# Attention and ternary feed-forward in one kernel: how h2's Strassen factors are made, when factors are fetched, and 96 bytes of padding

## The chip, the cores and the metric

The kernel runs on one core of a Trainium2 chip. A core has five engines that run their own instruction streams: TensorE (PE; its weight loads are shown as PEld), VectorE (DVE), ScalarE (ACT), GpSimd (POOL) and SyncE (SP, which here only issues DMAs). The metric is the device time of one execution in microseconds. Three runs of the kernel before gave 877.13, 877.68 and 878.19 us.

## The reference

The input x has 2 sequences of 2048 tokens with 256 features, all in fp32. The output is a residual sum of a causal attention and a feed-forward network, both on the normalised x:

```python
xn = layernorm(x)
q, k, v = xn @ Wq, xn @ Wk, xn @ Wv
attn = softmax(where(causal, q @ k.T, -max) * 256**-0.5) @ v @ Wo
h = silu((xn @ w1.T) * w1_s) * ((xn @ w2.T) * w2_s)      # 256 -> 1024
h = gelu((h @ h1.T) * h1_s)                              # 1024 -> 1024
h = gelu((h @ h2.T) * h2_s)                              # 1024 -> 1024
out = x + attn + (h @ w3.T) * w3_s                       # 1024 -> 256
```

The weights w1, w2, h1, h2 and w3 hold only -1, 0 and 1 in this input; their scales w1_s and so on are real numbers, one for each output feature.

## The kernel before, in words

**Blocks and passes.** The 4096 tokens are 8 blocks of 512. Attention comes first (to about 280 us). For each block it leaves two things in DRAM: xT_d, the normalised block with features on the partitions, split into a high and a low part so that two fp32r matmuls together are exact enough; and r_d, the attention's result. While it runs, it also looks through the feed-forward weights to see that they are ternary. If they are, ffn_ternary runs (L697), otherwise a general version (ffn) that the change leaves alone.

ffn_ternary goes over the blocks in pairs: four passes of an even block n and an odd block n + 1. The tile xh0 holds the even block's xn, xh1 (in the profile xh1t) the odd one's. xh0 is in the pool const, which is laid out first and stays for the whole kernel; xh1 is in a pool that is laid out after const, once attention's pools are gone, and so are the other tiles of ffn_ternary.

**One pass.** `first` (L728) computes the 1024 hidden features of both blocks as four quarters B11, B12, B22, B21: the first figure of the name picks the half of the features and the second the token block, so B11 and B21 use xh0, B12 and B22 use xh1. Each quarter has 4 tiles of 128 features by 512 tokens. For each tile PE makes two products of 4 matmuls (L741) in two PSUM banks, ACT applies silu (L746), DVE multiplies (L747), and what a later product needs is split into high and low parts by ACT (L724) and DVE (L725). The differences that Strassen's scheme (in Winograd's form) needs are made in t1 (L762, DVE), b22 (L767 on GpSimd, L768 on DVE) and later at L826 (GpSimd).

`square` (L773) then does a 1024 x 1024 layer with seven half-sized products instead of eight. The list STEPS (L39) gives for each of the seven the left factor, made of the weights, and the right one, made of the activations. The left factors of a layer lie in a DRAM tile, factors["h1"] and factors["h2"], as seven parts of 1 MB: part 0 is A11, parts 1 to 4 are the sums S1, S2, S4, S3, parts 5 and 6 are A12 and A22. A product fetches its factor into a tile w of a pool with three buffers (L781, L782) and runs 32 matmuls (L789). After h1 and h2 comes the last layer for both blocks (ps_y, L897), with the residual: rt (from r_d) and xt (from x) are loaded at L884 and L886 and added by GpSimd at L887.

**Making the factors of h2.** h1's factors are made during attention; of h2's weights, only the check of their values is done there. The parts of h2 are made in pass 1 by make_h2 (L852), once for each of 4 row groups c: two loads of 512 KB into the two staging tiles stgt (L856), four adds by GpSimd (L150) into a tile sums that has one buffer, and store_factors (L152): one store of the four sums (1 MB, L153) and three stores of 256 KB from the staging tiles (L154, L156) for the parts 0, 5 and 6, which are plain quarters of h2. load_w3 (L862) loads and rounds w3 in two halves. The list `later` holds these six steps in order; one is taken after B11, after B12, and after products 0, 2, 4 and 5 of the first layer (L756, L794).

**What sets the order.** The program is written in the order described, but a planner puts each engine's instructions into an order of its own: it estimates durations and gives an engine the earliest one in program order that it takes to be ready. Instructions that depend on nothing can so come far ahead of their place: rt and xt of pass 1 are issued at 287 us, though they belong at its end. On the chip each engine then works its own stream strictly in that order. All DMAs of ffn_ternary are issued by SP and so go into one queue.

## Time and profile before

| | |
|---|---|
| median of three runs | 877.68 us |
| the profiled execution | 877.43 us, its span 875.6 us |
| busy over the span | PE 854.3 us (98%), DVE 630.6 (72%), ACT 498.0 (57%), POOL 235.6 (27%) |
| feed-forward matmuls with xh / xh1t as moving operand (L741) | 256 each, 60.0 and 60.6 us busy |
| factor fetches (L782) | 56 of 1 MB, median 4.7 us from issue to landing |
| GpSimd's sums for h2 (L150) | 16, of 1.46 to 1.57 us on average |
| stores of h2's sums / of its quarters | 4 of 1 MB, median 8.0 us; 12 of 256 KB, median 5.9 us |

The profile is of one execution. Busy time of PE counts pipelined matmuls whose ends overlap, so that the pace of PE is read from the distance between starts, not from an instruction's duration. A timeline line gives start, duration of the group, engine, line, operation, output <- inputs, shapes and count; in square brackets how long the engine had sat idle before it and what is taken to have released it. Where that releaser had been done for long, the real one was something else, often a DMA.

### The profile page before, as it was taken

The numbers are of one execution on the slowest core, as the hardware profiler recorded it, in microseconds if no ns is written. First come the engines' busy times: TensorE is split into PE (matmuls) and PEld (weight loads), VectorE is DVE, ScalarE is ACT, GpSimd is POOL, SyncE is SP. The second block draws the span as 40 slices with busy tenths as digits, with TensorE's granted clock in tenths as the row PEclk, the third lists the DMA queues.
The fourth block names the chain that finished last, engine by engine and source line by source line (L and its number), as shares of the span: only waits on it lengthen the run. The fifth ranks groups of instructions, "written<-read, shape, count | busy, mean of one in ns | idle before, by whom it ended". The sixth has DMA issues, their size and how long they took to land.

```text
span 875.6 us, 12225 instructions
## 1 busy us (share of the span) xinstructions
PE 854.3 (98%) x4280; PEld 721.6 (82%) x4280; DVE 630.6 (72%) x1127; ACT 498.0 (57%) x881; POOL 235.6 (27%) x176
## 2 busy tenths in 40 slices
PE   8999999999998999999999999999999999999996
PEld 5888878988877877888988888888888898888886
DVE  5698689796873995985496596569468648848663
ACT  2546555754753664677266586536557635657670
POOL 4012533202121574440143050025024012502401
PEclk8999999999999999999999999999999999999998
DMA  8877599866892969744424444432434442144312
GB/s 305 326 229 242 168 321 293 302 236 200 238 325 91 365 239 378 258 147 145 139 90 146 147 144 145 156 125 99 144 144 145 147 142 97 49 144 145 144 49 77
DMA packets 63989, 162.51 MB, mean 186 GB/s; under 512 B 6704, under 2 KB 36528, under 8 KB 54704
## 3 DMA queue, kind: packets, MB, share of 16 engines
q1 hardware_dynamic: 58448, 145.92, 48.6%
q10 hardware_dynamic: 5472, 15.73, 5.6%
q8 instruction: 36, 0.59, 0.3%
q14 instruction: 33, 0.27, 0.1%
HBM read 117.06 MB, written 47.71 MB: 188 GB/s over the span
## 4 chain that ended last, share of the span: by engine, by line
PE 70%; DMA 13%; DVE 7%; issue 2%; ACT 2%; SPq 2%; POOL 2%; ACTq 0%; DVEq 0%; POOLq 0%
PE ps_h_X L789 26%; PE ps_w_B L741 13%; PE ps_h_Z L789 13%; PE ps_h_Y L789 7%; PE ps_y L897 6%; DMA e<-d 6%; DMA d<-b 4%; DMA stg<-in_ffn_h_w 2%; SPq L267 2%; DVE b L255 2%; PE pv L336 1%; PE po L443 1%; DVE stg L530 1%; POOL x L283 1%; DVE s L373 1%
## 5 line engine op out<-in xcount | busy, mean ns | idle before, releaser
L364 PE MATMUL pss<-k,q 128*128 128x512 f32 (+3 forms) x480 | 111.0, 369 | 3.1 <-DVE q L215 1.7
L364 PEld LDWEIGHTS pss<-k,q 128*128 128x128 f32 x480 | 81.8, 189 | 16.2 <-DVE q L215 2.1
L789 PE MATMUL ps_h_X<-h_h_T,w_h_S 128*128 128x512 f32 x384 | 89.0, 389 | 0.0
L789 PEld LDWEIGHTS ps_h_X<-h_h_T,w_h_S 128*128 128x128 f32 x384 | 72.1, 188 | 15.0
L443 PE MATMUL po<-v,pT 128*128 128x512 f32 x272 | 79.7, 405 | 3.0 <-ACT pT L423 1.9
L425 POOL TENSOR_TENSOR pT<-e,pT 128x512 fp32r<-128x512 f32 (+3 forms) x30 | 36.3, 1212 | 162.3 <-ACT pT L423 101.6
L887 POOL TENSOR_TENSOR rt<-rt,xt 128x1024 f32<-128x1024 f32 x8 | 19.7, 2458 | 216.5 <-DMA rt<-r_d 200.3
L810 ACT ACTIVATE k_h_u<-k_h_u,h_s_sb 128x512 f32<-128x512 f32 x64 | 46.1, 722 | 41.6 <-DVE k_h_u L809 41.4
L746 ACT ACTIVATE f_w_B<-ps_w_B,w_s_sb 128x512 f32<-128x512 f32 x64 | 42.8, 683 | 43.1 <-PE ps_w_B L741 43.1
L741 PE MATMUL ps_w_B<-xh,w_sb 128*128 128x512 f32 x256 | 60.0, 391 | 2.9 <-DVE f_w_B L747 1.6
L897 PEld LDWEIGHTS ps_y<-w_sbt,h_h_B 128*128 128x128 f32 x512 | 62.0, 192 | 0.3
L897 PE MATMUL ps_y<-w_sbt,h_h_B 128*128 128x256 f32 x512 | 62.1, 283 | 0.0
L423 ACT CAST pT<-e 128x512 fp32r<-128x512 f32 (+3 forms) x60 | 32.6, 573 | 49.6 <-DMA e<-d 38.3
L741 PE MATMUL ps_w_B<-xh1t,w_sb 128*128 128x512 f32 x256 | 60.6, 396 | 0.0
L789 PE MATMUL ps_h_Y<-h_h_B,w_h_A 128*128 128x512 f32 x256 | 59.3, 389 | 0.0
L789 PE MATMUL ps_h_X<-h_h_T,w_h_A 128*128 128x512 f32 x256 | 59.3, 389 | 0.0
L741 PEld LDWEIGHTS ps_w_B<-xh,w_sb 128*128 128x128 f32 x256 | 47.7, 188 | 13.4 <-DVE f_w_B L747 2.0
L443 PEld LDWEIGHTS po<-v,pT 128*128 128x128 f32 x272 | 49.0, 193 | 11.0 <-ACT pT L423 2.4
L741 PEld LDWEIGHTS ps_w_B<-xh1t,w_sb 128*128 128x128 f32 x256 | 48.1, 188 | 11.8
L789 PEld LDWEIGHTS ps_h_Y<-h_h_B,w_h_A 128*128 128x128 f32 x256 | 48.0, 188 | 10.0
L789 PEld LDWEIGHTS ps_h_X<-h_h_T,w_h_A 128*128 128x128 f32 x256 | 48.0, 188 | 10.0
L385 ACT ACTIVATE s<-s,low 128x1024 f32<-128x1024 f32 (+7 forms) x48 | 43.0, 898 | 21.3 <-DVE low L379 21.0
(139 smaller groups left out, 1845.3 us busy)
## 6 DMA issues: line engine op xcount, KB each, us to landing
w_h_S<-factors_h SPq DMA_DIRECT2D x32, 1024.0 KB, 4.7
w_h_A<-factors_h SPq DMA_DIRECT2D x24, 1024.0 KB, 4.7
d<-b SPq DMA_DIRECT2D x18, 512.0 KB, 4.3
e<-d SPq DMA_DIRECT2D x72, 128.0 KB, 4.1
xT_d<-k SPq DMA_DIRECT2D x8, 1024.0 KB, 8.7
stg<-in_ffn_h_w ACTq DMA_DIRECT2D x16, 512.0 KB, 6.5
x<-in_attn_x SPq DMA_DIRECT2D x16, 256.0 KB, 6.5
r_d<-r SPq DMA_DIRECT2D x8, 512.0 KB, 5.5
```

Source lines behind the costliest of these rows:

```text
L255: nc.vector.transpose(b.rearrange("p (g k q) -> p k g q", g=P // Q, q=Q), src.rearrange("p (k g q) -> p k g q", g=P // Q, q=Q),)
L364: nc.tensor.matmul(out=ps[:, :w], lhsT=qs[n][:, c, a, ts(t, P)], rhs=ks[m][:, c, b, :w], start=(k == 0), stop=(m < n and k == 3 * DC - 1),)
L385: marks["ACT"] = nc.scalar.activation(st["s"][:, at], st["s"][:, at], AF.Exp, bias=low, accum_out=st["sums"][:, u // UK : u // UK + 1],).ins
L423: nc.scalar.copy(hi, src)
L425: engine.tensor_tensor(lo, src, hi.bitcast(F32), ALU.subtract)
L443: nc.tensor.matmul(out=st["po"], lhsT=pT[:, 0, ts(j, P)], rhs=vs[m][:, j, :, :], start=(m == first and j == 0), stop=False,)
L741: nc.tensor.matmul(out=p, lhsT=w[:, c, ts(o, P)], rhs=xh[:, c, a, :], start=(c == 0 and a == 0), stop=(c == DC - 1 and a == 1),)
L746: nc.scalar.activation(f, p1, AF.Silu, scale=sc["w1"][:, o : o + 1])
L789: nc.tensor.matmul(out=out[o], lhsT=w[:, c, ts(o, P)], rhs=sets[right][c][:, a, :], start=(start and c == 0 and a == 0), stop=(c == HK - 1 ...
L810: nc.scalar.activation(C[k][o], r[o] if r else banks[o], AF.Gelu, scale=s[:, at : at + 1])
L887: nc.gpsimd.tensor_tensor(rest, rest, xt, ALU.add)
L897: nc.tensor.matmul(out=ys[t][:, :D], lhsT=h[c][:, a, ts(t, P)], rhs=w3_sb[:, c, :], start=(c == 0 and a == 0), stop=(c == HC - 1 and a == 1),)
```

## The change

Four things change, all but the first in ffn_ternary.

1. A tile of 24 floats per partition, named pad and used by nothing, is added at the end of const. Each tile laid out after const starts 96 bytes higher.
2. make_h2 stores the four sums only. The three plain quarters of h2 (parts 0, 5 and 6) are copied by copy_h2, one DMA of 1 MB each, from h2 in DRAM to factors["h2"] in DRAM, without a tile in between.
3. The steps sit at other places of pass 1, by name rather than in a list: make_h2(0) after B11, copy of part 0 after B12, make_h2(1) after B22, copy of part 5 after product 0 of h1, make_h2(2) after product 1, copy of part 6 after product 2, make_h2(3) after product 3, and the halves of w3 after products 5 and 6.
4. The factor tiles are fetched by fetch_factors, which keeps up to three of them asked for, across layers and passes. It is called once before pass 1, right after the load of xh1, and at the beginning of every product; a product takes the first of the list. In program order a fetch so stands two products ahead of its use. The pool still has three buffers.

```diff
     flag = const.tile([1, 1], I32, name="flag")
+    const.tile([P, 24], F32, name="pad")
...
-    def store_factors(f, c, sums, halves):
-        nc.sync.dma_start(out=f[:, 1:5, c, :], in_=sums)
-        nc.sync.dma_start(out=f[:, 0, c, :], in_=halves[0][:, :HB])
-        for i in range(2):
-            nc.sync.dma_start(out=f[:, 5 + i, c, :], in_=halves[1][:, ts(i, HB)])
...
-                if later and k in ("B11", "B12"):
-                    later.pop(0)()
+                beside(k)
...
-                left, right = STEPS[step]
-                w = wp.tile([P, HK, HB], F32R, tag="w", name=f"w_{name}_{left}")
-                nc.sync.dma_start(
-                    out=w.bitcast(F32).rearrange("p c o -> p (c o)"),
-                    in_=factors[layer][:, step].rearrange("p c o -> p (c o)"),
-                )
+                right = STEPS[step][1]
+                fetch_factors()
+                w = factor_tiles.pop(0)
...
-                if later and step in (0, 2, 4, 5):
-                    later.pop(0)()
+                if layer == "h1":
+                    beside(step)
...
-            store_factors(factors["h2"], c, sums, halves)
+            nc.sync.dma_start(out=factors["h2"][:, 1:5, c, :], in_=sums)
...
-        later = [lambda c=c: make_h2(c) for c in range(HK)]
+        def copy_h2(step):
+            k, o = {0: (0, 0), 5: (HK, 0), 6: (HK, HB)}[step]
+            nc.sync.dma_start(out=factors["h2"][:, step], in_=h2[:, ds(k, HK), ds(o, HB)])
+
+        later = {
+            "B11": lambda: make_h2(0), "B12": lambda: copy_h2(0), "B22": lambda: make_h2(1),
+            0: lambda: copy_h2(5), 1: lambda: make_h2(2), 2: lambda: copy_h2(6),
+            3: lambda: make_h2(3), 5: lambda: load_w3(0), 6: lambda: load_w3(SC // D),
+        }
+
+        def beside(at):
+            if at in later:
+                later.pop(at)()
+
+        factor_order = [
+            (layer, n, step) for n in range(0, N, 2) for layer in ("h1", "h2") for step in range(len(STEPS))
+        ]
+        factor_tiles = []
+
+        def fetch_factors():
+            while factor_order and len(factor_tiles) < 3:
+                layer, n, step = factor_order.pop(0)
+                w = wp.tile([P, HK, HB], F32R, tag="w", name=f"w_{layer}_{n}_{STEPS[step][0]}")
+                nc.sync.dma_start(
+                    out=w.bitcast(F32).rearrange("p c o -> p (c o)"),
+                    in_=factors[layer][:, step].rearrange("p c o -> p (c o)"),
+                )
+                factor_tiles.append(w)
+
         load_xh(1)
-        for c in range(0, HC, SC // D):
-            later.append(lambda c=c: load_w3(c))
+        fetch_factors()
```

More of the change, by code (lines that the diff above doesn't have):

```diff
@@ L865, in load_w3 @@
             rounded(w3_sb[:, c : c + SC // D, :].rearrange("p c d -> p (c d)"), t)
-        later = [lambda c=c: make_h2(c) for c in range(HK)]
+        def copy_h2(step):
[6 more added lines that the diff above has]
+        }
+        assert HK == 4 and HC == 2 * SC // D
+        def beside(at):
[14 more added lines that the diff above has]
+                factor_tiles.append(w)
         load_xh(1)
-        for c in range(0, HC, SC // D):
-            later.append(lambda c=c: load_w3(c))
+        fetch_factors()
         for n in range(0, N, 2):
```

## The prediction

> **What bounds the kernel now.** I read the page's header first, then the busy times by stage, then the chain that ended last, and then, where that chain leaves TensorE, the timelines of the engines concerned. The stages of the answer by windows are attention, the four passes of the feed-forward half (two token blocks each), and the tail; the columns are window, length, busy time and instruction count of PE, PEld, DVE, ACT, POOL, then clock, DMA share and GB/s.
>
> ```profile
> 0.00:279.70 279.70, 267.48 (x1464) 227.77 (x1465) 213.77 (x551) 151.40 (x297) 72.33 (x86) 0.98 0.78 251
> 279.70:429.00 149.30, 147.27 (x705) 123.55 (x706) 110.49 (x139) 87.56 (x147) 60.48 (x36) 1.00 0.68 247
> 429.00:575.50 146.50, 146.50 (x705) 123.49 (x705) 101.58 (x145) 86.72 (x146) 34.68 (x19) 1.00 0.39 137
> 868.50:875.60 7.10, 0.03 (x1) 0.00 (x0) 1.63 (x5) 0.00 (x0) 0.00 (x0) 0.68 0.24 81
> ```
>
> From 279.7 to 868.5 us TensorE sets the time: passes 2 to 4 have no idle PE at all and take 146.5 each. Pass 1 takes 149.3, of which PE is idle 2.03. So there are two things to win in this half: those 2 us, and the pace of single matmuls. The change touches neither attention's instructions nor the tail.
>
> The pace is read from the start times in PE's timeline of pass 2:
>
> ```profile
> 428.84 7.46 PE L741 MATMUL ps_w_B<-xh,w_sb 128*128 128x512 f32 x32
> 436.14 15.15 PE L741 MATMUL ps_w_B<-xh1t,w_sb 128*128 128x512 f32 x64
> 451.13 7.44 PE L741 MATMUL ps_w_B<-xh,w_sb 128*128 128x512 f32 x32
> 458.41 7.46 PE L789 MATMUL ps_h_X<-h_B,w_h_A 128*128 128x512 f32 x32
> 465.70 7.42 PE L789 MATMUL ps_h_Z<-h_T,w_h_S 128*128 128x512 f32 x32
> 472.96 1.30 PE L789 MATMUL ps_h_X<-h_T,w_h_S 128*128 128x512 f32 x5
> ```
>
> The same shape costs (472.96-465.70)/32 = 227 ns in the products, (436.14-428.84)/32 = 228 with the even block's xh as moving operand, but (451.13-436.14)/64 = 234 with the odd block's xh1t. Nothing waits there; the only difference is the tile.
>
> The two stalls of pass 1, from the timelines of PE, POOL, DVE and SP's queue:
>
> ```profile
> 310.19 1.21 PE L741 MATMUL ps_w_B<-xh,w_sb 128*128 128x512 f32 x4 [1.62 <-DVE f_w_B L747]
> ...
> 333.57 7.54 PE L789 MATMUL ps_h_Z<-h_B,w_h_S 128*128 128x512 f32 x32 [0.39 <-ACT h_h_T L724]
> ```
>
> ```profile
> 301.42 2.87 POOL L887 TENSOR_TENSOR rt<-rt,xt 128x1024 f32<-128x1024 f32 x1 [6.32 <-PE ps_w_B L741]
> 304.24 4.69 POOL L767 TENSOR_TENSOR f_w_B<-f_w_B,f_w_B 128x512 f32<-128x512 f32 x3
> ```
>
> ```profile
> 302.60 2.24 DVE L725 TENSOR_TENSOR h_B<-f_w_B,h_B 128x512 fp32r<-128x512 f32 x1
> 306.02 1.76 DVE L768 TENSOR_TENSOR f_w_B<-f_w_B,f_w_B 128x512 f32<-128x512 f32 x1 [1.19 <-POOL f_w_B L767]
> ```
>
> ```profile
> 323.99 0.37 SPq L153 DMA_DIRECT2D factors_h<-sums_h  x1
> 324.47 0.45 SPq L856 DMA_DIRECT2D stgt_h<-in_ffn_h_w  x1
> 325.00 0.98 SPq L782 DMA_DIRECT2D w_h_S<-factors_h  x1
> ```
>
> The first stall runs backwards so. PE lacks a PSUM bank until L747 has read it (309.40 to 310.14). That multiply stood behind L768, which waits for GpSimd's L767. L767 could have begun when f_w_B was there (302.69), but began at 304.24, because the residual add L887 was ahead of it on POOL. The add's wait is put down to PE, but its xt was issued at 287.48 and took 13.8 us to land, so 301.3: it was the DMA. The queue is full there (392 GB/s between 287 and 302, DMA share 1.00). The second stall is also a DMA: the step's matmul had its banks since 323.3, and ACT is a coincidence; its factor w (S4) was issued at 325.0 and took 8.4 us, so 333.4. The slot was free at 318.5, when product 0 ended; SP stood behind the store of h2's second sums, which waited for GpSimd until 323.99.
>
> **What the Trainium skill says.** "TensorE: Matmul & The Clock Gate", Step-by-step: PE has two independent SBUF read ports, and loading the next weights takes no bandwidth from the running matmul. The trace does not quite agree: 234 against 227 ns. The built addresses of the kernel before are the hint: w1_sb at byte 16512 and xh0 at 32896 are multiples of 64; xh1t at 50464 is 32 past one. In the products both operands are 32 past one, and they run at 227: slow is the mixed pair, not the odd address. "SBUF — State Buffer", SBUF: two separate sides: DVE and GpSimd share a port pair as an exclusive lock, and the loser waits for the whole instruction. It agrees: the split L725 takes 0.68 us alone and 1.77 to 2.24 beside GpSimd. "DMA: Bandwidth & Descriptors", Queues, rings and completion order: an engine consumes a queue's descriptors in ring order. It agrees: xt, behind 5 MB, took 13.8 us, and 3.6 to 4.4 are the medians for these loads over the run.
>
> **The change part by part.** The sum is against the profiled execution: 877.43, of which 875.6 span and 1.83 around it. The median of the runs shown, 877.68, lies 0.25 above.
>
> *Padding.* 24 floats of 96 bytes move all later tiles: xh1t goes from 50464 to 50560 = 790 x 64. It then agrees with w1_sb modulo 64 (both are 128 modulo 256). Attention's operands move together, so none of their differences changes. Gain per pass: 29.57 us (429.00 to 458.57 in the chain) less 128 x 0.2269 = 29.04, so 0.53; four passes 2.1. Bounds: 0 if the tile's address isn't the cause; 2.2 at most. The queries' matmuls pq, whose operands differ by 64 modulo 128, run between at about 229: if such a rest stayed, 64 x (234-229) x 4 = 1.3. I take 2.1. Is there room for PE to go faster? Its cover is DVE: in pass 2 the bank of X's first matmul (458.41) was freed by L747 at 457.11, so 1.3 us are left and 0.53 are used. No stall.
>
> *Quarters by copies.* Out go 12 stores of 256 KB (L154, L156); in come three 1 MB copies. The bytes are equal, 3 MB. SP's DMAs for h2 fall from 24 to 15; at 0.33 to 0.5 us each this is some 3 us of issue, hidden while SP idles. The staging tiles no longer wait for stores (SP's L856 waited 11.3 us for them), only for the sums. The copies depend on nothing, so the planner will issue them early: the like copies of h1 (L544, L546) went out at 1.7 to 19.9 us, far ahead of their place. Here they fall into the full queue after 280 us, ahead of rt and xt in program order: 3 x 2.67 us (1 MB at the window's 392 GB/s is 2.67) = 8 us more ahead of xt.
>
> *Factors ahead.* In the trace they are already fetched ahead: three at 285.27 to 286.9, and the next pass's first ones before its y stage. What changes is rank. At the start three come before h2's loads: r_d, xh1t, 3 factors, 2 x 0.5 MB = 5.5 MB x 2.67 = 14.7 us from 279.5, plus about 1.5 to land: 295.7, where the sums began at 288.69 before. They took 6.4 us, so they end at 302.1, just before L767 is wanted (302.69). And S4 ranks ahead of later h2 work: issued from 318.5, it lands by 327. I take the 0.39 as gone (between 0 and 0.39).
>
> *Sums at other places.* 16 adds of 1.5 us, 24 us of POOL, stay the same in number. Sums 1 move behind B22, 2 and 3 behind products 1 and 3; the first product to use them starts at 369.96, over 20 us later, so their lateness costs nothing. Sums 0 now lock DVE's port at 295.7 to 302 instead of 288.7 to 295: 2.5 us of DVE delay (the three long DVE operations then took 4.56 against 2.05), which DVE enters with as much less backlog. The residual add, with xt landing at 306 or later, should be planned behind the first L767, which then starts at 302.7 instead of 304.24; 1.55 us earlier removes nearly the whole 1.62. Bounds for this stall: gain 1.62, loss 6 (below). Since the sums end with 0.6 us to spare, I take half: 0.9.
>
> Sum: 2.1 + 0.9 + 0.35 = 3.35; 877.43 - 3.35 = 874.1, and against the median 874.3.
>
> **The rivals.** (1) *The stall stays*, because the sums or their lock on DVE reach past 302.7. For it: the 0.6 us of margin rests on a landing I worked out. Against: DVE is ahead by then. 877.68 - 2.1 = 875.6, between 875 and 876.3. (2) *The residual add wedges POOL*, the slower side: it is still ahead of L767 on GpSimd, and xt, behind 3 MB of copies, lands at 307.5. L767 then starts at 310.4, 6.1 later; the stall grows by as much: 877.7 + 6.1 - 2.1 - 0.35 = 881.3. It decides from xt landing after 303.9 (301.4 + 2.45). For it: copies rank ahead of xt, and the queue is full. Against: the order on POOL follows the planner's estimate, which sees the same queue and would then put a ready L767 first. (3) *The padding does nothing*, because the tile isn't moved or 64 bytes isn't what counts: 877.7 - 1.25 = 876.4.
>
> **How the numbers follow.** Forecast 0.58 (872.8 to 875.3), rival 1 0.17, rival 2 0.15 (with any reordering that opens a stall in passes 2 to 4), rival 3 0.10. One measurement tells no less than 0.2%, 1.75 us: faster is below 875.9, slower above 879.4. Faster: 0.58, of rival 1 0.13, of rival 3 0.03: 0.74. Slower: rival 2, 0.15. Same: 0.11. The range 872.0 to 879.0 leaves out rival 2 and little else.
>
> **What would show it.** xh1t's 64 matmuls at 14.5 instead of 15.0 us in passes 2 to 4, and those passes at 146.0; the three copies near 281 to 290 us; sums 0 starting near 296; L767 starting near 302.7 with the add behind it; S4 landing before 330. Wrong would make it: 234 ns at xh1t still, an L887 ending after 305 ahead of L767, or an idle PE in a later pass.

## The result and the profile after

The changed kernel takes 873.06 us, the median of 12 runs (870.58 to 877.31), against 877.74 for the kernel before (12 runs, 876.22 to 879.20): ratio 0.9951, 95% interval 0.9937 to 0.9966. The profiled execution took 872.97 us with a span of 871.1.

The line numbers have moved by the diff: the matmuls on xn are now L736 (L741 before), silu L741, DVE's multiply L742 (L747), split L720 (L725), GpSimd's and DVE's differences L761 and L762 (L767, L768), products L780 (L789), factor fetches L885 (L782), h2's loads L847 (L856), the copies L860, rt, xt and the residual add L905, L907 and L908 (L884, L886, L887).

The stages of the kernel after, by windows (window, length, then busy time and instructions of PE, PEld, DVE, ACT, POOL, then clock, DMA share, GB/s). Attention ended at 278.2 us here:

```profile
278.20:426.00 147.80, 146.87 (x705) 123.28 (x706) 111.05 (x139) 87.82 (x147) 60.65 (x36) 1.00 0.69 249
426.00:571.90 145.90, 145.90 (x706) 123.43 (x705) 101.85 (x144) 86.66 (x146) 34.79 (x19) 1.00 0.39 137
571.90:717.90 146.00, 146.00 (x707) 123.53 (x706) 101.68 (x144) 86.76 (x146) 34.17 (x19) 1.00 0.40 137
```

From its first matmul to that of the next pass, pass 1 takes 147.82 us here and took 149.11 before; passes 2 and 3 have lost about 0.6 each and still have no idle PE. Where passes 2 to 4 lost it is seen in PE's timeline of pass 2 of the kernel after:

```profile
433.26 14.67 PE L736 MATMUL ps_w_B<-xh1t,w_sb 128*128 128x512 f32 x64
447.77 7.42 PE L736 MATMUL ps_w_B<-xh,w_sb 128*128 128x512 f32 x32
455.02 7.42 PE L780 MATMUL ps_h_X<-h_B,w_h_A 128*128 128x512 f32 x32
```

(447.77-433.26)/64 = 226.7 ns on xh1t, where it was 234.2. In pass 1, from PE's timeline of the kernel after:

```profile
300.02 7.42 PE L736 MATMUL ps_w_B<-xh,w_sb 128*128 128x512 f32 x32
307.56 7.55 PE L780 MATMUL ps_h_X<-h_B,w_h_A 128*128 128x512 f32 x32
315.63 7.57 PE L780 MATMUL ps_h_Z<-h_T,w_h_S 128*128 128x512 f32 x32 [0.52 <-DVE f_w_B L742]
...
337.99 7.52 PE L780 MATMUL ps_h_X<-h_h_T,w_h_S 128*128 128x512 f32 x32 [0.28 <-DMA w_h_S<-factors_h]
```

The stall of 1.62 us within the third stretch (xh) is gone, and so is the wait of product 2. In their place stand a wait of 0.52 ahead of Z (product 1) and one of 0.28 ahead of product 4. The engines behind them, first POOL after:

```profile
294.04 1.30 POOL L151 TENSOR_TENSOR sums_h<-stgt_h 128x512 f32<-128x512 f32 x1 [25.86 <-DMA stgt_h<-in_ffn_h_w]
...
300.41 4.68 POOL L761 TENSOR_TENSOR f_w_B<-f_w_B,f_w_B 128x512 f32<-128x512 f32 x3
307.59 1.67 POOL L761 TENSOR_TENSOR f_w_B<-f_w_B,f_w_B 128x512 f32<-128x512 f32 x1 [2.50 <-DVE f_w_B L742]
309.23 2.84 POOL L908 TENSOR_TENSOR rt<-rt,xt 128x1024 f32<-128x1024 f32 x1
```

The residual add now stands behind all four L761. But DVE pays for it there, as its timeline after shows (two splits for T2 beside the add, and the same two in pass 2, with no add):

```profile
309.74 3.48 DVE L720 TENSOR_TENSOR h_T<-f_w_B,h_T 128x512 fp32r<-128x512 f32 x2
...
456.71 1.28 DVE L720 TENSOR_TENSOR h_T<-f_w_B,h_T 128x512 fp32r<-128x512 f32 x2
```

And SP after: the fetch of 328.56 stands behind a store that waited for GpSimd, and its factor is the one product 4 waits for.

```profile
325.88 0.33 SPq L847 DMA_DIRECT2D stgt_h<-in_ffn_h_w  x1
327.58 0.37 SPq L851 DMA_DIRECT2D factors_h<-sums_h  x1
328.05 0.46 SPq L847 DMA_DIRECT2D stgt_h<-in_ffn_h_w  x1
328.56 0.42 SPq L885 DMA_DIRECT2D w_h_S<-factors_h  x1
```

### The profile page after: what moved, and what is told of

Its sections match the earlier page's. It is cut to its first block, busy times and chain, and to the rows that moved or that the text cites. A ratio compares the mean times of both kernels' runs of the same rounds, so it can differ in the third digit from the quotient of the medians.

```text
span 871.1 us, 12211 instructions
## 1 busy us (share of the span) xinstructions
PE 851.1 (98%) x4280; PEld 720.7 (83%) x4280; DVE 630.3 (72%) x1127; ACT 498.2 (57%) x881; POOL 236.3 (27%) x176
## 4 chain that ended last, share of the span: by engine, by line
PE 61%; DMA 3%; POOL 1%; DVE 1%; issue 0%; SPq 0%; DVEq 0%; POOLq 0%
PE ps_h_X L780 26%; PE ps_h_Z L780 13%; PE ps_w_B L736 10%; PE ps_h_Y L780 7%; PE ps_y L918 6%; DMA stgt_h<-in_ffn_h_w 1%; DMA w_h_S<-factors_h 1%; POOL sums_h L151 1%; DVE f_w_B L762 0%; DMA rt<-r_d 0%; POOL rt L908 0%; DVE h_B L720 0%; DMA out<-yt 0%; POOL f_w_B L761 0%; DVE f_w_B L742 0%
## 5 line engine op out<-in xcount | busy, mean ns | idle before, releaser
L780 PE MATMUL ps_h_X<-h_h_T,w_h_S 128*128 128x512 f32 x384 | 89.1, 389 | 0.3 <-DMA w_h_S<-factors_h 0.3
L780 PEld LDWEIGHTS ps_h_X<-h_h_T,w_h_S 128*128 128x128 f32 x384 | 72.0, 188 | 15.6 <-ACT k_h_u L801 0.7
L908 POOL TENSOR_TENSOR rt<-rt,xt 128x1024 f32<-128x1024 f32 x8 | 19.6, 2453 | 209.9 <-DMA rt<-r_d 209.9
L741 ACT ACTIVATE f_w_B<-ps_w_B,w_s_sb 128x512 f32<-128x512 f32 x64 | 43.0, 684 | 43.5 <-PE ps_w_B L736 43.5
L736 PE MATMUL ps_w_B<-xh,w_sb 128*128 128x512 f32 x256 | 59.5, 390 | 1.3 <-DVE r L457 1.3
L780 PE MATMUL ps_h_X<-h_h_T,w_h_A 128*128 128x512 f32 x256 | 59.3, 389 | 0.0
L780 PE MATMUL ps_h_Y<-h_h_B,w_h_A 128*128 128x512 f32 x256 | 59.3, 389 | 0.0
L736 PE MATMUL ps_w_B<-xh1t,w_sb 128*128 128x512 f32 x256 | 58.7, 389 | 0.0
L736 PEld LDWEIGHTS ps_w_B<-xh,w_sb 128*128 128x128 f32 x256 | 47.8, 188 | 11.2 <-issue 1.5
L780 PEld LDWEIGHTS ps_h_Y<-h_h_B,w_h_A 128*128 128x128 f32 x256 | 48.0, 188 | 10.0
L780 PEld LDWEIGHTS ps_h_X<-h_h_T,w_h_A 128*128 128x128 f32 x256 | 48.0, 188 | 10.0
L736 PEld LDWEIGHTS ps_w_B<-xh1t,w_sb 128*128 128x128 f32 x256 | 48.0, 188 | 10.0
L380 ACT ACTIVATE s<-s,low 128x1024 f32<-128x1024 f32 (+7 forms) x48 | 43.0, 897 | 20.3 <-DVE low L374 19.9
```

The lines of the kernel that those rows point to most:

```text
L380: marks["ACT"] = nc.scalar.activation(st["s"][:, at], st["s"][:, at], AF.Exp, bias=low, accum_out=st["sums"][:, u // UK : u // UK + 1],).ins
L736: nc.tensor.matmul(out=p, lhsT=w[:, c, ts(o, P)], rhs=xh[:, c, a, :], start=(c == 0 and a == 0), stop=(c == DC - 1 and a == 1),)
L741: nc.scalar.activation(f, p1, AF.Silu, scale=sc["w1"][:, o : o + 1])
L780: nc.tensor.matmul(out=out[o], lhsT=w[:, c, ts(o, P)], rhs=sets[right][c][:, a, :], start=(start and c == 0 and a == 0), stop=(c == HK - 1 ...
L908: nc.gpsimd.tensor_tensor(rest, rest, xt, ALU.add)
```

## How the experiments are read

Totals of one kernel spread over 5 to 9 us from run to run, and a ratio is good to 0.1 to 0.35%, which is 1 to 3 us. Passes 2 to 4 are far steadier: with the same addresses, every stretch of them agrees between profiles to 0.01 us. So two things are taken from each experiment. The first is the length of each pass and stretch, from start to start in PE's timeline (first matmul on xh to the next pass's, and to the last y matmul for pass 4). The second is the ratio of the totals. Their difference (the ratio's change times 878.5 us, less the change of the four passes) is what happened outside the passes: attention, and a tail of 7.1 to 9.9 us. It is no better than the ratio, 1 to 3 us.

Pass 1 is less steady than the later ones. In the eight kernels that leave its program as it was, it takes 1.5 to 2.8 us longer than the same kernel's pass 2 (2.60 in the kernel before). In the two profiles of the changed program, with and without padding, it is 1.88 and 2.13. A difference of less than about 1 us in one profile of pass 1 thus doesn't tell two programs apart; a wait that comes or goes in all profiles of a program does.

Totals also go with the clock that TensorE was granted. Over the 329 runs on record, a run whose mean clock is 0.001 lower than that of another run of the same kernel is about 0.6 us longer (a fit). In the profiles the clock falls to a half in two or three stretches of 3.4 or 6.8 us of attention, and in the passes of one kernel only.

| kernel | ratio to before, 95% interval | pass 1 | pass 2 | four passes, us against before | ratio's change in us | outside the passes |
|---|---|---|---|---|---|---|
| before | | 149.11 | 146.51 | | | |
| after | 0.9951 (0.9937 to 0.9966) | 147.82 | 145.94 | -3.0 | -4.3 | -1.3 |
| padding alone | 0.9956 (0.9941 to 0.9972) | 148.57 | 145.94 | -2.3 | -3.9 | -1.6 |
| after, no padding | 1.0000 (0.9980 to 1.0019) | 148.64 | 146.51 | -0.5 | 0.0 | +0.5 |
| xh1t moved alone | 0.9976 (0.9961 to 0.9991) | 148.19 | 145.77 | -3.1 | -2.1 | +1.0 |
| padding of 32 bytes | 0.9986 (0.9965 to 1.0006) | 148.72 | 146.41 | -0.7 | -1.2 | -0.5 |
| padding of 224 bytes | 0.9967 (0.9953 to 0.9980) | 148.16 | 146.38 | -1.3 | -2.9 | -1.6 |
| attention's tiles moved | 0.9965 (0.9948 to 0.9982) | 148.33 | 146.25 | -1.6 | -3.1 | -1.5 |
| b and e moved | 0.9990 (0.9978 to 1.0002) | 149.34 | 146.51 | +0.2 | -0.9 | -1.1 |
| hpt moved | 1.0121 (1.0086 to 1.0156) | 150.75 | 149.23 | +9.8 | +10.6 | +0.8 |
| after, old places | 0.9946 (0.9928 to 0.9963) | 148.26 | 145.94 | -2.6 | -4.7 | -2.1 |
| after, late factors | 0.9917 (0.9888 to 0.9946) | 146.49 | 145.94 | -4.3 | -7.3 | -3.0 |
| after, no copies | 0.9984 (0.9967 to 1.0000) | 150.45 | 145.94 | -0.4 | -1.4 | -1.0 |
| after, reordered | 1.0003 (0.9984 to 1.0023) | 153.63 | 145.52 | +1.6 | +0.3 | -1.3 |

## Experiments on the padding

**Padding alone.** The kernel before plus one line:

```diff
+    const.tile([P, 24], F32, name="pad")
```

> The kernel before plus the padding tile alone. Theory (place of xh1t against the weights sets the pace of its matmuls): the 64 matmuls on xh1t take 14.5 us in each pass, 227 ns each, where they took 15.0 at 234; passes 2 to 4 come to 146.0 us against 146.5; pass 1 keeps its two stalls of 1.62 and 0.39 us; the whole 1.6 to 2.1 us below the kernel before. Rival (the padding does nothing, and the shorter passes come from the other parts): passes of 146.5, 234 ns, total unchanged. On attention: if the padding moved it, its end lies near 278.2 us as in the changed kernel; if that was variation from run to run, it lies anywhere between 278 and 280.

Passes 2 to 4 are those of the changed kernel, 145.94 us. In pass 2 of this kernel, PE's timeline, (448.90-434.39)/64 = 226.7 ns:

```profile
434.39 14.67 PE L742 MATMUL ps_w_B<-xh1t,w_sb 128*128 128x512 f32 x64
448.90 7.42 PE L742 MATMUL ps_w_B<-xh,w_sb 128*128 128x512 f32 x32
```

Nearly the whole difference between before and after is there: 0.9956 against 0.9951. That is 3.9 us where 1.6 to 2.1 were expected, and the passes make 2.3 of it. The first stall is still there but 1.21 us, not 1.62, and the wait of product 2 is 0.57. Attention ended at 278.54 in this profile; a single profile settles nothing, since the kernels that leave attention where it was ended anywhere from 279.7 to 282.6.

**The changed kernel without the padding** (the same line taken out).

> The changed kernel without its padding. Theory: xh1t's matmuls back to 234 ns and passes 2 to 4 to 146.5 us, while pass 1 keeps what the moved sums and the earlier factors saved (X h1 follows without the 1.62 us stall, its second stall stays near 0.3); total about 2 us above the changed kernel, near 875. Rival (padding does nothing): passes of 145.9 and a total of 873.

xh1t's matmuls are back at 234.2 ns and passes 2 to 4 at 146.51 us. The total is 878.40, not the 875 expected: without the padding the other three parts together change nothing that the runs can tell (0.9980 to 1.0019). Pass 1 is 0.47 us shorter than before in this profile, which is less than it varies. Pass 1 has the changed kernel's pattern, with 0.54 us ahead of Z; product 3's stretch, at whose end product 4 waits for its factors, was 8.28 us here and 7.70 in the changed kernel.

**xh1t moved alone** (with the pools behind it). The kernel before with the 96 bytes in the feed-forward half only:

```diff
         w3_sb = fw.tile([P, HC, D], F32R, name="w3_sbt")
+        fw.tile([P, 24], F32, name="pad")
         xh1 = fw.tile([P, DC, 2, TB], F32R, name="xh1t")
```

> The kernel before with the same 96 bytes put behind w3_sbt and ahead of xh1t, so that attention's tiles lie where they lay before and only xh1t and what follows it are moved. Theory (only xh1t's own place counts in the passes): passes 2 to 4 at 146.0 us as with the padding in front. If padding also changed attention, this kernel's attention ends near 279.7 while that with the padding in front ends near 278.2; if not, the two ends differ only as runs do. Rival: passes of 146.5.

xh1t's matmuls take 226.7 ns, as expected. Passes 2 to 4 are even shorter than after, 145.77: here y's 128 matmuls take 15.19 us in place of 15.35, because w3_sbt stays and hpt moves (more below). Yet the total falls only to 0.9976: outside the passes this kernel is 2.6 us behind the one with the padding in front (+1.0 against -1.6). That is a sign that the padding does something in attention too.

**Which distance counts.** The kernel with the padding alone, with 8 floats (32 bytes) instead of 24, and in a second kernel with 56 (224 bytes):

```diff
-    const.tile([P, 24], F32, name="pad")
+    const.tile([P, 8], F32, name="pad")
```

> The kernel before with padding of 8 floats: xh1t at byte 50496, 789 times 64, and so an odd multiple of 64 away from the weights' place modulo 128. If what counts is the place modulo 64, xh1t's matmuls take 227 to 229 ns and passes 2 to 4 come to 146.0 to 146.2 us; if it is modulo 128, they stay at 231 to 234 ns and the passes at 146.4 to 146.5. If padding does nothing, 146.5 as well, which the first run tells apart.

> The kernel before plus padding of 224 bytes instead of 96: xh1t at byte 50688, 0 modulo 256 where the weights lie at 128 modulo 256, and attention's tiles at 0 modulo 128 as with 96 bytes. With 32 bytes the matmuls on xh1t stayed at 233.6 ns. If the period is 128 bytes, xh1t's matmuls take 227 ns and passes 2 to 4 come to 145.9 us; if it is 256 or more, they stay above 229 ns and the passes above 146.1. On attention (a multiple of 128 bytes shortens its 1 KB transfers): the mean 1 KB packet of attention near 58 ns against 61 before, and the total some 4 us below the kernel before; rival (attention's shorter stretch with the 96 bytes was chance): packets at 61 ns and a total lower by the passes' 2.3 us alone.

Both stay slow, 233.6 and 233.4 ns. Pass 2 of the kernel with 224 bytes, PE's timeline, where (451.90-436.98)/64 = 233.1:

```profile
436.98 15.09 PE L742 MATMUL ps_w_B<-xh1t,w_sb 128*128 128x512 f32 x64
451.90 7.44 PE L742 MATMUL ps_w_B<-xh,w_sb 128*128 128x512 f32 x32
```

From the built addresses, the place of xh1t less that of w1_sb, modulo 256, and the mean pace over the kernel:

| xh1t less w1_sb, modulo 256 | 160 (before) | 192 (32 bytes) | 128 (224 bytes) | 32 (attention's tiles moved) | 0 (after; xh1t moved alone) |
|---|---|---|---|---|---|
| ns for one matmul | 234.2 | 233.6 | 233.4 | 233.7 | 226.7 |

Agreeing modulo 64 or 128 is not enough: 256 bytes is the smallest power of two that fits all five. The 24 floats reach it because the distance was 160 and they add 96.

**The distance, or the tile?** The kernel before with 32 bytes put between the factors' tiles and the right operands of the fourteen products:

```diff
         wp = actx.enter_context(tc.tile_pool(name="wpt", bufs=3))
+        sh = actx.enter_context(tc.tile_pool(name="sht", bufs=1))
+        sh.tile([P, 8], F32, name="shim")
         stgp = actx.enter_context(tc.tile_pool(name="stgpt", bufs=2))
```

> The kernel before with 32 bytes put between the factors' pool (wpt) and the pools behind it, so that the right operands (hpt) lie 32 bytes away from the factors modulo 128, where they lay 0 away. Theory (the distance of the two operands modulo 128 sets the pace): the 448 matmuls of the fourteen products take 234 ns in place of 227, a pass grows by 448 x 7.2 ns = 3.2 us to 149.7, the whole by 12.9 us to about 890; xh1t stays at 234. Rival (only xh1t's tile has the trouble, for a reason of its own, or only its own place counts): the products stay at 227 ns and passes at 146.5.

The total is 890.07 us, where about 890 was expected. Pass 2 of this kernel, PE's timeline:

```profile
460.42 7.62 PE L791 MATMUL ps_h_X<-h_B,w_h_A 128*128 128x512 f32 x32
467.88 7.63 PE L791 MATMUL ps_h_Z<-h_T,w_h_S 128*128 128x512 f32 x32
```

(467.88-460.42)/32 = 233.1 ns in a product that ran at 227. Of a product's two operands only the right one was moved. In the kernel with 32 bytes of padding both were, the right one to the same place, and a product took 7.25 us as before. So it is the distance between the operands that sets the pace here, not the place of one. A pass grew by 2.72 us and not 3.2: a product grew by 0.21 us and not 0.23, and y's matmuls became quicker, from 15.35 to 15.14 us. Why the distance counts, no run shows.

The rule is shown for the feed-forward matmuls. In attention the score matmuls (pss, 128x512) are a mixture in both kernels, some 40% within 228 ns of the one before and most others 229 to 240; nothing here takes that apart.

## Experiments on attention

The padding in front moves attention's tiles too, from 32 past a multiple of 128 to a multiple of 128. Two kernels take that apart. The first has the padding in front, and 32 bytes more ahead of xh1t, so that its matmuls stay slow:

```diff
+    const.tile([P, 24], F32, name="pad")
...
+        fw.tile([P, 8], F32, name="pad_fw")
         xh1 = fw.tile([P, DC, 2, TB], F32R, name="xh1t")
```

> The kernel before with the 96 bytes of padding in front of attention's tiles and 32 bytes more ahead of xh1t, so that attention's tiles lie as in the changed kernel but xh1t lies 32 bytes past a multiple of 128 again. Passes 2 to 4 at 146.5 us in every theory. Theory (the place of attention's tiles is worth time of its own): total 2 to 2.5 us below the kernel before, 1 KB packets of attention at 58 ns on the mean. Rival (it is not; attention's shorter stretch was chance, or the whole gain belongs to xh1t): total as before within 0.5 us, packets at 61 ns.

The second moves attention's pool bp by 96 bytes. The pool holds the tile b, which goes out to DRAM, and e, which comes back by transfers of 1 KB pieces. What lies behind it moves by 128 bytes, and so keeps its place modulo 128, but not modulo 256:

```diff
+        sh1 = actx.enter_context(tc.tile_pool(name="sh1", bufs=1))
+        sh1.tile([P, 24], F32, name="shim1")
         bp = actx.enter_context(tc.tile_pool(name="bp", bufs=2))
+        sh2 = actx.enter_context(tc.tile_pool(name="sh2", bufs=1))
+        sh2.tile([P, 8], F32, name="shim2")
```

> The kernel before with 96 bytes of padding in attention only, right ahead of the pool of b and e (the tiles that the 1 KB transfers read and fill), and 32 bytes behind it, so that b and e lie at multiples of 128 and every other tile keeps its place modulo 128. Passes at 146.5 us. Theory (the destination of the 1 KB transfers into e is what counts): packets at 58 ns on the mean, attention and total 2 to 2.5 us shorter. Rival (another tile's place, or chance): packets at 61 ns and total unchanged.

With attention's tiles moved the passes came to 146.25 and not to 146.5 us, again through y (w3_sbt and hpt moved apart by 32 bytes). What is left outside the passes is -1.5 us. With b and e moved it is -1.1, and the interval of the total just includes no change.

This second kernel is not as clean as it was meant to be, and shows the rule of 256 bytes once more. The tile pT, weights of attention's matmuls on v (po), lies behind bp and so moved by 128 bytes against v. Of the po matmuls of 512 columns 36 to 41% start within 228 ns of the one before in each of the other thirteen kernels, and 7% in this one; their mean is 234.9 ns where it was 232.9. For 272 of them that is 0.5 us at most, an estimate, which hides as much of the gain.

A single kernel does not settle it. In the nine kernels whose b and e lie at multiples of 128, the last column of the table is -1.0 to -3.0, -1.6 on average; in the four that have them elsewhere it is -0.5 to +1.0. But the granted clock is a rival. If the totals are compared by their means and corrected by 0.6 us for each 0.001 of clock (an estimate; seven of the nine have what it needs), the two sets lie at -0.3 to -1.6 and -0.5 to +1.4, some 1.1 us apart on average, and they overlap. Attention's ends in the single profiles overlap too, 278.2 to 282.1 us against 279.7 to 282.6. Whether the clock is higher by chance or because attention waits less is not shown.

The trace's records of the 15,488 packets of 1 KB in attention part without overlap:

```
mean ns of a 1 KB packet before 278 us
b and e elsewhere:          before 61.4   no padding 60.7   xh1t alone 61.2   32 bytes 61.0   hpt moved 60.3
b and e at multiples of 128: after 57.5   padding alone 58.6   224 bytes 56.6   attention's tiles 57.9   b and e 59.3
                             old places 58.6   late factors 58.4   no copies 59.8   reordered 58.7
```

The median is 46 ns in every kernel. What differs are the slower packets: three quarters are done within 71 to 74 ns where b and e lie elsewhere, and within 59 to 69 where they lie at multiples of 128. By their sizes, 9,216 of the packets go into e and nearly all others into the tiles of x, which the kernel with b and e moved leaves where they were; that it has about half of the packets' gain fits.

So padding in front makes attention's 1 KB packets shorter on the mean, and probably attention by 1 to 2 us. That the packets are the cause is argued, not shown. The busy times of ACT's and DVE's large groups in attention show no step between the two sets; they are the same to a few per cent but for DVE's share of the pT splits (20.9 to 25.9 us).

The Trainium skill has a page that bears on it: "DMA: Bandwidth & Descriptors", How a descriptor splits into AXI transactions, says that a piece is cut at the multiples of 256 bytes, and that a start off such a multiple fetches bytes that it doesn't use. It speaks of reading, and what moved here is where the pieces of e are written. The only kernel with e at a multiple of 256 (224 bytes of padding) has the shortest packets, 56.6 ns, as if it held for writing too. But worked out by that page, an estimate, 1 KB from 128 past such a multiple needs 36 beats of 32 bytes and from 32 past one 33, so the former should be the slower, and measured it is the quicker (57.5 to 59.8 against 60.3 to 61.4). A cost of each packet would also move the median, which stays. So no run here shows that rule to be the cause.

## Experiments on pass 1

Three kernels undo one part each of the changed kernel. Each column is from one profile, each stretch from start to start, in us; the last column is the steady value of pass 2 of the changed kernel.

| stretch of pass 1 | before | padding alone | after | old places | late factors | no copies | reordered | steady |
|---|---|---|---|---|---|---|---|---|
| xh, third stretch | 9.19 | 8.76 | 7.54 | 7.69 | 7.25 | 7.28 | 7.50 | 7.25 |
| product 0 (X) | 7.27 | 7.26 | 8.07 | 8.09 | 7.25 | 9.07 | 7.38 | 7.25 |
| product 1 (Z) | 7.25 | 7.25 | 7.41 | 7.43 | 7.25 | 7.39 | 7.25 | 7.25 |
| product 2 | 7.81 | 7.99 | 7.25 | 7.25 | 7.25 | 7.25 | 7.25 | 7.25 |
| product 3 | 7.38 | 7.37 | 7.70 | 7.90 | 7.40 | 7.25 | 7.25 | 7.25 |
| product 4 | 7.25 | 7.25 | 7.36 | 7.36 | 7.36 | 9.38 | 7.25 | 7.25 |
| h2, product 0 | 7.25 | 7.25 | 7.25 | 7.25 | 7.25 | 7.25 | 12.24 | 7.25 |
| h2, product 1 | 7.25 | 7.25 | 7.25 | 7.25 | 7.25 | 7.25 | 9.74 | 7.25 |

**Old places.**

```diff
-            "B11": lambda: make_h2(0), "B12": lambda: copy_h2(0), "B22": lambda: make_h2(1),
-            0: lambda: copy_h2(5), 1: lambda: make_h2(2), 2: lambda: copy_h2(6),
-            3: lambda: make_h2(3), 5: lambda: load_w3(0), 6: lambda: load_w3(SC // D),
+            "B11": lambda: make_h2(0), "B12": lambda: (copy_h2(0), make_h2(1)),
+            0: lambda: (copy_h2(5), make_h2(2)), 2: lambda: (copy_h2(6), make_h2(3)),
+            4: lambda: load_w3(0), 5: lambda: load_w3(SC // D),
```

> The changed kernel with the sums of h2 made at their old places (beside B11, B12 and the first and third products, w3 beside the fifth and sixth), copies, early factors and padding kept. In its program GpSimd's order around the first matmuls is the changed kernel's: sums 0, the four subtractions for T1's successor, then the residual add. Theory (that order, which the moved places do not make, removes the first stall): no stall before the last four xh matmuls, the third xh stretch 7.5 us, X 8.1, pass 1 near 147.8. Rival (the prediction's step: the new places remove it): the stall of 1.2 to 1.6 us is back and pass 1 near 149.

GpSimd's order is the same with the old places, and the 1.62 us stall does not come back; 0.27 us of it do, and product 4 waits 0.49. Pass 1 is 148.26 - 147.82 = 0.44 us longer than in the changed kernel, which is less than it varies: the same program without padding took 148.64, with 8.28 for product 3. That the new places are worth anything is not shown.

**Late factors.**

```diff
-            while factor_order and len(factor_tiles) < 3:
+            while factor_order and len(factor_tiles) < 1:
...
         load_xh(1)
-        fetch_factors()
```

> The changed kernel with each product's factors fetched when the product is written, as before, and the rest kept. Theory (the early fetch took the 0.4 to 0.6 us wait of product 2 away, and gave 0.3 to 0.45 of it back at product 3, whose factors now come late): product 2's stretch 7.8 us in place of 7.25, product 3's 7.3 to 7.4 in place of 7.70, pass 1 within 0.2 us of 147.8. Rival (the early fetch is worth its whole 0.35): product 3 stays at 7.7, pass 1 near 148.2.

Both expectations missed. Product 2 has no wait without the early fetch either, and pass 1 comes to 146.49 us, the shortest of all. It exceeds this kernel's pass 2 by 0.55 us, where the changed program has 1.88 and 2.13. So the early fetch costs about 1.3 us of pass 1, by one profile. PE's timeline of this kernel runs through:

```profile
303.08 7.42 PE L736 MATMUL ps_w_B<-xh,w_sb 128*128 128x512 f32 x32
310.34 7.42 PE L780 MATMUL ps_h_X<-h_B,w_h_A 128*128 128x512 f32 x32
317.59 7.42 PE L780 MATMUL ps_h_Z<-h_T,w_h_S 128*128 128x512 f32 x32
324.84 7.42 PE L780 MATMUL ps_h_X<-h_T,w_h_S 128*128 128x512 f32 x32
332.10 7.41 PE L780 MATMUL ps_h_Z<-h_B,w_h_S 128*128 128x512 f32 x32
```

The reason is on SP and POOL of the same kernel, whose pass 1 began at 281.00. SP:

```profile
284.37 0.81 SPq L847 DMA_DIRECT2D stgt_h<-in_ffn_h_w  x2
285.33 0.69 SPq L860 DMA_DIRECT2D factors_h<-in_ffn_h_w  x1
286.15 0.53 SPq L885 DMA_DIRECT2D w_h_A<-factors_h  x1
```

and POOL:

```profile
289.56 1.30 POOL L151 TENSOR_TENSOR sums_h<-stgt_h 128x512 f32<-128x512 f32 x1 [19.76 <-DMA stgt_h<-in_ffn_h_w]
...
301.26 5.08 POOL L761 TENSOR_TENSOR f_w_B<-f_w_B,f_w_B 128x512 f32<-128x512 f32 x3 [5.75 <-DVE f_w_B L742]
308.83 1.69 POOL L761 TENSOR_TENSOR f_w_B<-f_w_B,f_w_B 128x512 f32<-128x512 f32 x1 [2.49 <-DVE f_w_B L742]
310.47 2.85 POOL L907 TENSOR_TENSOR rt<-rt,xt 128x1024 f32<-128x1024 f32 x1
```

The loads of h2 go ahead of the factors, so the first sums start 8.6 us after the start of the pass; in the changed kernel they stand behind 3 MB of factors and start 15.9 after it, and until 22.3 they hold DVE back (its difference and its split of 0.68 us took 1.79 and 1.78 there). The first L761 then starts 20.3 instead of 22.3 us into the pass, the add 29.5 instead of 31.1. The add holds DVE's splits just as long here (3.48 us for two), but DVE comes to them 30.0 us into the pass and not 31.6.

**No copies.** store_factors is back, and the keys "B12", 0 and 2 are gone:

```diff
             nc.sync.dma_start(out=f[:, 1:5, c, :], in_=sums)
+            nc.sync.dma_start(out=f[:, 0, c, :], in_=halves[0][:, :HB])
+            for i in range(2):
+                nc.sync.dma_start(out=f[:, 5 + i, c, :], in_=halves[1][:, ts(i, HB)])
```

> The changed kernel with the quarters of h2 stored from the staged halves again, three stores beside each store of sums, and no DRAM to DRAM copies; new places, early factors and padding kept. In its program the residual add stands ahead of the four subtractions again. Theory (the copies, which load SP's queue ahead of xt, made the order and so the gain): the stall of 1.2 to 1.6 us before the last xh matmuls is back, X back to 7.3, pass 1 at 148.6 or more. Rival (the prediction: copies are worth nothing): pass 1 at 147.8, no stall before the last xh matmuls.

Pass 1 is 150.45 us: undoing the copies costs 2.63 in this profile. The order on POOL is the expected one, with the add ahead of the four L761:

```profile
301.02 2.86 POOL L912 TENSOR_TENSOR rt<-rt,xt 128x1024 f32<-128x1024 f32 x1
303.83 6.85 POOL L761 TENSOR_TENSOR f_w_B<-f_w_B,f_w_B 128x512 f32<-128x512 f32 x4
```

The stall came, though not where it was expected: PE's timeline of this kernel has it inside X and ahead of Z, and a new one at a fetch of factors.

```profile
310.26 5.75 PE L780 MATMUL ps_h_X<-h_B,w_h_A 128*128 128x512 f32 x24 [0.28 <-DVE f_w_B L742]
317.05 7.55 PE L780 MATMUL ps_h_Z<-h_T,w_h_S 128*128 128x512 f32 x32 [1.05 <-DVE f_w_B L742]
...
348.32 3.91 PE L780 MATMUL ps_h_Y<-h_h_B,w_h_A 128*128 128x512 f32 x16 [1.97 <-DMA w_h_A<-factors_h]
```

The last of these makes most of the 2.63. On SP the fetch of A12 stands behind a store of sums that waited for GpSimd until 337.2; it was issued at 338.20 and took 10.0 us to land, where the changed kernel issued it at 330.49. X's stretch is 1.0 us longer than in the changed kernel, the one before it 0.26 shorter. No run adds the copies alone to the kernel before.

**Reordered.** An attempt at a better version, with the first pair's residual add ordered behind the last sums, h2's loads behind the newest fetch of factors (for which a product also calls fetch_factors a second time, after its matmuls), and w3_sbt moved by 32 bytes against hpt:

```diff
+                fetch_factors()
                 if layer == "h1":
                     beside(step)
...
+                with tc.issue_after(last_sum[0]) if m == 1 else nullcontext():
                     nc.gpsimd.tensor_tensor(rest, rest, xt, ALU.add)
...
+                with tc.issue_after(last_fetch[0]):
                     nc.sync.dma_start(out=t, in_=h2[:, k, :])
...
+        fw.tile([P, 8], F32, name="pad3")
         w3_sb = fw.tile([P, HC, D], F32R, name="w3_sbt")
+        fw.tile([P, 56], F32, name="pad4")
         xh1 = fw.tile([P, DC, 2, TB], F32R, name="xh1t")
```

> The changed kernel with three edits: the residual add of the first pair of blocks is ordered behind the last sums of h2; the loads of h2 are ordered behind the newest fetch of factors; w3_sbt moved by 32 bytes and xh1t by 256, so that only w3_sbt changes its place modulo 256 against hpt. Theory: without the add beside it VectorE is not held, X's stretch in pass 1 goes from 8.07 to 7.3 us; product 3's from 7.70 to 7.3; y's 128 matmuls from 15.35 to 15.15 in each pass as in the three kernels where w3 and h differed modulo 256; pass 1 near 146.5, passes 2 to 4 at 145.75, total about 2 us below the changed kernel, near 871 beside 878 before. Rivals: the add was not what held VectorE (X stays at 8.1), or the add now holds up the xt load behind it and with it w3 or h2's factors, seen as a new wait in products 7 to 9.

The stretches it was aimed at became as short as expected, and the time was lost elsewhere. X's stretch is 7.38 us: the first sums are as late as in the changed kernel (16.0 us into the pass), and without the add beside DVE there is no wait. In the kernel with late factors the add is there, the sums are early, and there is no wait either. So the 0.52 needs both, late sums and the add. Product 3 is at 7.25 and y at 14.94. But h2's product 1 waits for its factor:

```profile
373.31 9.90 PE L783 MATMUL ps_h_Z<-h_h_T,w_h_S 128*128 128x512 f32 x32 [4.83 <-DMA w_h_S<-factors_h]
```

POOL and SP of this kernel say why. The last loads of h2, now behind a fetch, landed for sums that started at 352.67, and the add went in between them. The store of those sums at 361.90 is what the factors' fetch at 367.47 reads.

```profile
352.67 1.29 POOL L152 TENSOR_TENSOR sums_h<-stgt_h 128x512 f32<-128x512 f32 x1 [10.11 <-DMA stgt_h<-in_ffn_h_w]
353.92 2.85 POOL L915 TENSOR_TENSOR rt<-rt,xt 128x1024 f32<-128x1024 f32 x1
```

```profile
361.90 0.38 SPq L856 DMA_DIRECT2D factors_h<-sums_h  x1
362.37 0.46 SPq L860 DMA_DIRECT2D stgt_w<-in_ffn_w_w  x1
367.47 1.36 SPq L891 DMA_DIRECT2D w_h_S<-factors_h  x3
```

The 4.83 us cost 7.5, since after the wait the product itself took 9.74 us and not 7.25: the trace has the granted clock at a half from 371.5 to 378.3 us, and the product's first matmuls start 427 ns apart instead of 227. That is the rival which named a wait for h2's factors, with another carrier: the loads' new order besides the add.

The shortest kernel is thus probably the changed one with late factors: 872.81 us in four runs, 0.9917 (0.9888 to 0.9946) of before. The changed kernel's interval overlaps its own; the passes, 1.3 us shorter, speak for it. Late factors with y's new distance were not run together.

## Why the prediction was right, and where not

The predicted time was 874.3 us, 3.35 below; measured are 873.06 and 4.7 below. The sum is right within the spread, its terms are not: in pass 1 gains booked at the wrong place and losses not foreseen nearly met, which is luck.

**Padding, -2.1: right in the passes.** 14.51 us for the 64 matmuls where 14.5 was said, 145.94 for a pass where 146.0 was said, no stall in passes 2 to 4; the padding alone takes 2.3 from the four passes. The reason given was only half right. "It then agrees with w1_sb modulo 64" is not what counts, for 192 and 128 modulo 256 are as slow as 160; the aside "both are 128 modulo 256" is. The sentence of the page "TensorE: Matmul & The Clock Gate" that loading weights takes no bandwidth from the running matmul does not lead one to expect this: 32 bytes of distance between moving operand and weights, and 233.1 ns for 227. Whether bandwidth is what is lost, no run shows.

**"Attention's operands move together, so none of its differences changes": a term of zero that was not zero.** It is true of the matmuls, and the prediction took it to hold for attention as a whole. But attention's transfers got new places too. Outside the passes the changed kernel became 1.3 us shorter by the ratio and 1.7 by the medians (4.7 less 3.0), and nine kernels against four say that 1 to 2 us go with the new place, with the granted clock as an open rival. This is the difference between 3.35 and 4.7; the passes gave 3.0.

**Sums at other places, -0.9: the right events under the wrong head.** Sums 0 were to start 16.0 us into the pass and did so at 15.9; L767 was to start 23.0 into it and started at 22.3; the add was to stand behind, and the stall in the third stretch fell by 1.65 us. But the moved places did not do it, for with the old ones it is gone too. The copies put the add there: it is behind in every profile of the planner's own order with copies, and ahead in the kernel before and in the changed one without copies. And it was not said that the add, once behind, would hold DVE's splits for T2, 3.48 us for 1.28. The step "which DVE enters with as much less backlog" failed: sums 0 late and the add late together make the wait ahead of Z, and X's stretch gave 0.80 us back.

**Quarters by copies, 0: wrong.** Undoing them costs 2.63 us of pass 1. Some 2.0 of it is the wait for A12's fetch, which the prediction did not name. For the rest it saw the way (8 us more of queue ahead of xt, the add planned later) and booked its fruit elsewhere.

**Factors ahead, -0.35: wrong in sign.** Product 2's wait did go, but it is gone with late factors too, because S4's fetch stands ahead of h2's loads (317.78 us) there as well. The early fetch costs 1.33 us in the two profiles compared, by the very 3 MB ahead of h2's first loads that the prediction counted, and priced only as far as the landing.

Pass 1 apart from xh1t's matmuls was to gain 1.25 and gained 0.8: -1.65 in the third stretch, +0.80 at X, +0.16 at Z, -0.56 at product 2, +0.32 and +0.11 at products 3 and 4. Each of these events is in both profiles of the changed program and in none of the program before, but their sum is smaller than pass 1 varies, and without the padding the total does not move: the net gain of the three parts is not shown to differ from nothing. They do not add up singly either, for each was measured with the others in place.

**The rivals.** That the stall stays: it went, and half as much came back at the next place. Whether pass 1 gained anything by it, these profiles do not tell. That the add wedges POOL: it did not, since the planner put it behind; without the copies it is ahead again, and pass 1 is 1.3 us longer than before. That the padding does nothing: no.

## What to carry to other kernels

When one tile's matmuls are a few per cent slower than others of the same shape, compare the built addresses of the two operands: here the feed-forward matmuls of 512 columns ran at full pace only where the operands agreed modulo 256 bytes, and a padding of the right size was worth more than the three reorderings together. A padding moves everything behind it, so transfers and other stages are part of its price, and a tile that was meant to stay can lose its own good distance. An early fetch is not free because its buffer is: price what it is put ahead of in the queue, and then what that late transfer's consumer collides with.

## What was not expected of the hardware

- Feed-forward matmuls of 512 columns: 226.7 ns with operands equal modulo 256 bytes, 233.1 to 234.2 at distances of 32, 128, 160 and 192. Attention's po matmuls: 36 to 41% within 228 ns, and 7% once their operands had been moved by 128 bytes against each other.
- Matmuls of 256 columns (y, with hpt as weights and w3_sbt moving) go the other way: 119.9 ns where both agree modulo 256, 118.7, 118.3 and 116.7 where w3_sbt less hpt is 160, 224 and 32. A y stretch took 15.35 us in the first case and 14.94 in the last.
- 1 KB packets in attention: 56.6 to 59.8 ns on the mean with b and e at multiples of 128 bytes, 60.3 to 61.4 with them elsewhere, and a median of 46 in all.
- In a wait of PE of 4.83 us the granted clock went to a half, for 6.8 us in all, and the first matmuls after the wait started 427 ns apart instead of 227.
